# Mamba layer: side work on TensorE one matmul at a time, from two rows with one PSUM bank each

## The chip, the core and the metric

The kernel runs on one core of a Trainium2 chip. A core has TensorE (PE: matrix products into PSUM, an accumulator memory of eight banks), VectorE (DVE), ScalarE (ACT) and GpSimd (POOL) for elementwise work, and SyncE (SP), which here issues the DMAs. Each engine works through its own queue in order and waits on semaphores. The metric is the device time of one execution in microseconds (us); lower is better.

## The reference

Four layers follow each other on an input of 2 images of 256 channels and 48x48 = 2304 positions. The change touches only the first, a bidirectional Mamba layer. For each image: layer norm and a position table; an input projection to `xi` and `z` of 512 channels each; and then for each direction `s` (forward `f`, backward `b`):

```
xs    = silu(conv4(xi) + conv_b)               # depthwise, 4 taps
proj  = xs @ xproj_w.T                         # 16 values for dt, 16 B, 16 C
dt    = softplus(proj[:, :16] @ dtproj_w.T + dt_b)
h_t   = exp(dt_t * A) * h_(t-1) + dt_t * xs_t * B_t     # 512 channels x 16 states
y_t   = sum over the 16 states of h_t * C_t, plus xs_t * D
out_s = y * silu(z)
```

The two directions' sums are added, multiplied with silu(z), projected back to 256 channels and added to the input. The later layers (attention and convolutions, a graph gate with experts, a mixture of experts) are left out here.

## The kernel before

**Pieces and tiles.** The 2304 positions are cut into six chunks of 384. A *piece* is one chunk of one image in one direction: 24 pieces, in the order image 0 forward, image 0 backward, image 1 forward, image 1 backward (pieces 0 to 5, 6 to 11, 12 to 17, 18 to 23). A piece has 64 *state tiles*: 16 states times 4 blocks of 128 channels. `layer0` walks over them one by one, tile `k`, and issues for each:

- `decay(k + 4)`: ScalarE, `he = exp(dt * A)` (L573).
- `turn_b(k + 2)`: TensorE, three 128x128 transposes of `dbt` (dt, xs and B multiplied, positions on partitions) into a bank `db`, one of three (L583). `dbt` itself is made by GpSimd two groups of four tiles ahead (`scale_b`, L563).
- the scan of tile `k` on VectorE: it reads `he` and `db` (L678 forward, L680 backward). In three groups out of four it writes `ho`, and after every second tile GpSimd multiplies the pair with C into `hcp` (L687); in the fourth VectorE itself does this into `hc` (L694). ScalarE keeps the last column as `state` for the next chunk.
- `add_state`, `POOL_LAG` = 8 or `DVE_LAG` = 2 tiles later: TensorE turns the product back and adds it to three open sums `y0` to `y2` in PSUM (L608).

**The sums.** `begin` opens the three sums at tile 6 of a piece with the D term (L598, twelve matmuls) and, backward, the forward sum (L593, three matmuls); `end` empties them at tile 5 of the next piece.

**Side work.** Beside the tiles run generators, each with a number of steps, a first and a last tile: `prepare` of the next piece (convolution L305, `xproj` L323, `dt` L340, softplus, transposes of `dtu` L370), `project_in` of a later chunk (layer norm, L238 and L249), `project_out` of the last backward piece (L386, L392), and, once the input projection is done (piece 10 on), `head_products` and `contexts`, which prepare later layers. After each tile every generator is advanced until it has caught up with its line:

```python
                slot = k - k0 + 1
                for e in beside:
                    steps, n_steps, s0, s1, _ = e
                    while e[4] * (s1 - s0) < n_steps * (slot - s0) and next(steps, e) is not e:
                        e[4] += 1
```

A step holds up to six matmuls; two or more generators may step in one tile. All take their banks from one ring of two (`ps`, tag `mm`). PSUM's eight banks: three `db`, two `mm`, three `y`.

**The order on the engines** is not quite that of the program: the framework's scheduler places each engine's instructions when the kernel is built, by program order and by when it reckons their inputs ready, and may move a matmul past others. So the place of each instruction is read from the built programs here, not from the source.

**Before the first tile** the chunks 0 and 1 of image 0 are projected and piece 0 is prepared, one behind the other; the other ten chunks are projected beside pieces 0 to 9.

Of the kernel before, what the change touches and what calls it, by code (L numbers as in the profile page):

```python
# [18 lines left out]
F32 = mybir.dt.float32  # L19
# [8 lines left out]
P = 128  # L28
# [135 lines left out]
def layer0(ctx, E):  # L164
# [4 lines left out]
    TILES = NS * DB  # L169
    D = DB * P  # L170
    EXP_AHEAD, DB_AHEAD, POOL_LAG, DVE_LAG = 4, 2, 8, 2
# [5 lines left out]
    ps = ctx.enter_context(tc.tile_pool(name="l0ps_s", bufs=2, space=PSUM))  # L177
# [14 lines left out]
    def bank():  # L192

        pool, tag = (ps, "mm") if scanning else (psd, "db")
        return pool.tile([P, D], F32, tag=tag, name="mm")

    def hold():

        return bank()[:, :W]

    def project_in(b, c):
# [7 lines left out]
        yield  # L209
        mp = hold()  # L210
        for k in range(2):
            nc.tensor.matmul(mp, lhsT=E.mean_c, rhs=h[:, k, :], start=k == 0, stop=k == 1)
        nc.vector.tensor_tensor(h, h, bc(mp, [P, 2, W], 1), ALU.subtract)
        sq = up.tile([P, 2, W], F32, tag="sq", name="sq")
        nc.scalar.activation(sq, h, AF.Square)
        yield
        vp = hold()
        for k in range(2):
            nc.tensor.matmul(vp, lhsT=E.mean_c, rhs=sq[:, k, :], start=k == 0, stop=k == 1)
        rs = up.tile([P, 2 * C], F32, tag="rs", name="rs")[:, :W]  # L220
# [5 lines left out]
        yield  # L226
        nc.vector.reciprocal(rs, rs)
        yield
        nc.vector.tensor_tensor(h, h, bc(rs, [P, 2, W], 1), ALU.mult)
        for k in range(2):  # L230
            nc.vector.scalar_tensor_tensor(
                h[:, k, :], h[:, k, :], E.v("ln_g", k, 1), pos[:, k, :], ALU.mult, ALU.add
            )
        yield
        for m in range(DB):
            px = hold()
            for k in range(2):
# [3 lines left out]
                )  # L241
            xz = wp.tile([P, D], F32, tag="xz", name="xz")[:, :W]
            nc.scalar.copy(xz, px)
            nc.sync.dma_start(xi_d[b][:, m, 3 + c * W : 3 + (c + 1) * W], xz)
            yield
        for j in range(TB):
            pz = bank()
            for k in range(2):
# [3 lines left out]
                )  # L252
            xz = wp.tile([P, D], F32, tag="xz", name="xz")
            nc.scalar.copy(xz, pz)
            nc.sync.dma_start(z_d[b][:, c, j], xz)
            yield
# [34 lines left out]
    def prepare(b, s, step, c, got):  # L291
# [7 lines left out]
        yield  # L299
        xs = wp.tile([P, DB, W], F32, tag="xs", name="xs")  # L300
        for d in range(DB):
            px = hold()
            for k in range(4):
# [5 lines left out]
                if k == 1:  # L309
                    yield  # L310
# [5 lines left out]
            yield  # L316
# [3 lines left out]
        yield  # L320
        pj = hold()
        for d in range(DB):
# [3 lines left out]
            if d == 1:  # L326
                yield
# [5 lines left out]
        yield  # L333
# [4 lines left out]
        for d in range(DB):  # L338
            pd = hold()
# [5 lines left out]
            yield  # L345
        nc.scalar.activation(ex, ex, AF.Exp, scale=-1.0)
        pb = bank()
# [3 lines left out]
        yield  # L351
# [5 lines left out]
        yield  # L357
        nc.vector.tensor_tensor(dt, dt, ln, ALU.add)
        yield
# [3 lines left out]
        yield  # L363
        yield
        yield
        dtt = wp.tile([P, TB, D], F32, tag="dtt", name="dtt")
        for j in range(TB):
            pt = bank()
# [3 lines left out]
            yield  # L372
        got[-1].update(dt=dt, dtt=dtt, bt=bt)
        yield

    N_PREPARE = 27

    def project_out(b, c, yt):
# [3 lines left out]
        g = up.tile([P, DB, W], F32, tag="u", name="g")  # L382
        for j in range(TB):
            pg = bank()
# [3 lines left out]
            yield  # L388
        for m in range(2):
            po = hold()  # L390
            for d in range(DB):
# [4 lines left out]
                if d == 1:  # L396
                    yield
            nc.vector.tensor_tensor(xo[:, m, :], xo[:, m, :], po, ALU.add)
            yield
# [3 lines left out]
        yield  # L403

    N_OUT = 8

    def head_products():
# [3 lines left out]
        for h, m, z in [(h, m, z) for h in range(3) for m in range(2) for z in range(2)]:  # L411
# [8 lines left out]
            yield  # L420
            pg = ps.tile([P, 2 * C], F32, tag="mm", name="pg")
            for k in range(3):
                nc.tensor.matmul(
                    pg, lhsT=w_eo[k][:, m * P : (m + 1) * P], rhs=w_eo[k], start=k == 0, stop=k == 2
                )
            if z == 0:
# [5 lines left out]
            yield  # L432
            pu = ps.tile([P, 2 * C], F32, tag="mm", name="pu")
            for i in range(2):
                o = i * C + m * P
                for k in range(3):
# [3 lines left out]
                    )  # L440
            ub = E.ub[:, h, m, :]
# [5 lines left out]
            yield  # L447

    def contexts():
# [13 lines left out]
        yield  # L463
# [11 lines left out]
        for c in range(NCH):  # L475
            xn = normed(c)
            yield
# [6 lines left out]
            for t in range(3):  # L484
                pk = ps.tile([P, 2 * C], F32, tag="mm", name="pk")
                for k in range(2):
# [3 lines left out]
                    )  # L490
                nc.tensor.matmul(pk, lhsT=E.mean_c[0:1, :], rhs=bkv, start=False, stop=True)
                nc.scalar.activation(kv[t][0], pk[:, :C], AF.Relu)
                nc.scalar.copy(kv[t][1], pk[:, C:])
                yield
            pc = ps.tile([P, C], F32, tag="mm", name="pc")
            for m in range(2):
                ms = slice(m * P, (m + 1) * P)
                for t in range(3):
                    nc.tensor.matmul(
                        pc[:, ms], lhsT=kv[t][0][:, ms], rhs=kv[t][1][:, ms], start=t == 0, stop=t == 2  # L500
                    )
            if c == 0:
# [3 lines left out]
            yield  # L506
        cx = cx.rearrange("p (m w) -> p m w", m=2)
        nc.vector.tensor_tensor(cx, cx, bc(E.hmask, [P, 2, P], 1), ALU.mult)
        for c in range(NCH):
            xn = normed(c)  # L510
            yield
            q = up.tile([P, 2, W], F32, tag="h", name="q")
            for m in range(2):
                pq = hold()
                for k in range(2):
# [3 lines left out]
                    )  # L519
# [14 lines left out]
    for steps in (first, project_in(0, 1)):  # L534
        run(steps)
# [1703 lines left out]
```

## Time and profile before

| | |
|---|---|
| median of 3 runs | 5252.86 us (5251.17 to 5254.41) |
| the profiled execution | 5300.51 us, span 5298.4 us |
| layer 0: first scan, last scan | 110.4 us, about 2404 us |
| a piece, from its first scan to the next piece's | 92 to 105 us (piece 0: 81, piece 23: 72) |
| TensorE busy, 100 to 2400 us | 82% to 90% of each 100 us |
| VectorE busy, the same | 74% to 92% |
| GpSimd busy, the same | 80% to 98% |
| ScalarE busy, the same | 56% to 82% |

An engine's busy time counts from start to end of each instruction. TensorE's matmuls overlap in its pipeline, so its busy share says little of what it could still take; the spacing of their starts says more. An entry of the trace such as `L583 PE MATMUL db<-ident,dbt x3` is three instructions of line 583 that write `db`; `<-PE db L583` behind a time is what ended an engine's idling before it. A matmul of float32 operands shows as two records, a transpose as one.

### The profile page before, as it was taken

To read this page: it belongs to the slowest core of one execution; us is meant where nothing else is said; L and a number is where in the kernel's file an instruction comes from. 1 tells how busy PE (TensorE), PEld (TensorE's weight loads), DVE (VectorE), ACT (ScalarE), POOL (GpSimd) and SP (SyncE) were. 2 spreads that over 40 slices of the span, in tenths; PEclk is the share of its full clock that TensorE was granted. 3 is DMA by queue.
4 is the path that set the end of the run, shared out by engine and by line. 5 is a ranking of instruction groups with operands and counts; after the bars stand their busy time and mean duration, and the time that the engine had idled before them with its cause. 6 is when DMAs were issued, how large, how long until landed. Compare 5 with 4: busy or idle time off the path is not lost. (4 is left out here: it accounts for less than half of the span.)

```text
span 5298.4 us, 61375 instructions
## 1 busy us (share of the span) xinstructions
PE 4818.9 (91%) x22242; PEld 3163.5 (60%) x22242; DVE 3273.5 (62%) x4801; ACT 2416.2 (46%) x4604; POOL 2444.2 (46%) x2091
## 2 busy tenths in 40 slices
PE   7888898898888898888999999999799999999897
PEld 4666666666666666665555555566455555555675
DVE  3888878877877778888999344466524410212344
ACT  4777777766667677662232223422033322222221
POOL 2998988878888888892000000058312100000331
PEclk8999999999999999999999999999889999999899
DMA  2222222222121122213110000111021100000322
GB/s 93 73 82 79 82 84 90 91 77 83 64 75 49 60 76 77 71 61 116 40 36 32 2 17 0 48 34 28 9 96 48 48 6 6 7 9 8 81 86 97
DMA packets 156376, 294.15 MB, mean 56 GB/s; under 512 B 29495, under 2 KB 108347, under 8 KB 155804
## 3 DMA queue, kind: packets, MB, share of 16 engines
q1 hardware_dynamic: 147356, 277.37, 15.4%
q0 software_dynamic: 8704, 12.73, 1.5%
q8 instruction: 179, 2.93, 0.2%
q14 instruction: 137, 1.12, 0.1%
HBM read 211.97 MB, written 78.07 MB: 55 GB/s over the span
## 5 line engine op out<-in xcount | busy, mean ns | idle before, releaser
L687 POOL TENSOR_TENSOR hcp<-ho,cc 128x768 f32<-128x768 f32 x576 | 1067.9, 1855 | 186.6 <-DVE ho L680 101.5
L583 PE MATMUL db<-ident,dbt 128*128 128x128 f32 x4608 | 795.6, 287 | 173.4 <-DVE ho L678 63.7
L563 POOL TENSOR_SCALAR dbt<-dtt,bt 128x512 f32<-128x512 f32 x1152 | 882.8, 782 | 116.4 <-PE db L583 114.4
L583 PEld LDWEIGHTS db<-ident,dbt 128*128 128x128 f32 x4608 | 555.7, 146 | 448.9 <-issue 119.5
L608 PE MATMUL y<-ident,hcp 128*128 128x128 f32 x3456 | 570.2, 276 | 47.0 <-POOL hcp L687 46.9
L573 ACT ACTIVATE he<-dt,negab 128x384 f32<-128x384 f32 x768 | 463.5, 614 | 172.2 <-DVE ho L680 111.6
L573 ACT ACTIVATE he<-dt,negaf 128x384 f32<-128x384 f32 x768 | 460.1, 613 | 166.0 <-DVE ho L678 105.1
L680 DVE TENSOR_TENSOR_SCAN ho<-he,state,db 128x384 f32<-128x384 f32 x480 | 457.6, 998 | 117.3 <-PE db L583 95.4
L678 DVE TENSOR_TENSOR_SCAN ho<-he,state,db 128x384 f32<-128x384 f32 x480 | 456.9, 997 | 111.5 <-PE db L583 89.6
L608 PEld LDWEIGHTS y<-ident,hcp 128*128 128x128 f32 x3456 | 418.2, 142 | 56.9 <-POOL hcp L687 51.7
L2042 POOL DMA_INDIRECT xe<-xt_d,token x48 | 47.5, 990 | 757.6 <-issue 713.5
L1977 PE MATMUL po<-at,xtok 128*128 128x384 f32 x864 | 329.5, 506 | 8.2 <-ACT at L1975 8.1
L1975 ACT ACTIVATE at<-sp 128x384 f32<-128x384 f32 x216 | 104.8, 491 | 467.2 <-PE sp L1968 467.1
L1968 PE MATMUL sp<-qT,xn 128*128 128x384 f32 x864 | 317.2, 486 | 0.0
L1615 PE MATMUL ph<-xn,w 128*128 128x384 f32 x768 | 292.6, 522 | 20.7 <-issue 6.8
L1173 POOL PARTITION_ALL_REDUCE most<-most x1 | 0.4, 422 | 619.4 <-DVE most L1172 619.4
L305 PE MATMUL mm<-xw,w_cv 128*128 128x384 f32 x768 | 283.3, 493 | 0.0
L1619 ACT ACTIVATE hid<-ph,vec 128x384 f32<-128x384 f32 x192 | 110.6, 581 | 340.3 <-PE ph L1615 247.1
L904 PE MATMUL pf<-t,wfc 128*128 128x384 f32 x768 | 254.9, 487 | 2.9 <-ACT hid L908 2.8
L1977 PEld LDWEIGHTS po<-at,xtok 128*128 128x128 f32 x864 | 149.9, 189 | 177.4 <-ACT at L1975 108.4
L923 PE MATMUL po<-hid,wfc 128*128 128x384 f32 x768 | 253.6, 486 | 0.0
L1615 PEld LDWEIGHTS ph<-xn,w 128*128 128x128 f32 x768 | 148.2, 202 | 133.2 <-issue 48.6
(481 smaller groups left out, 8819.4 us busy)
## 6 DMA issues: line engine op xcount, KB each, us to landing
cc<-bcd SPq DMA_DIRECT2D x96, 768.0 KB
xw<-xi_d SPq DMA_DIRECT2D x24, 774.0 KB
w<-in_m_w SPq DMA_DIRECT2D x16, 1024.0 KB
y_d<-y SPq DMA_DIRECT2D x32, 384.0 KB
ye<-y_d SPq DMA_DIRECT2D x32, 384.0 KB
xi_d<-xz SPq DMA_DIRECT2D x48, 192.0 KB
z_d<-xz SPq DMA_DIRECT2D x36, 256.0 KB
y<-z_d SPq DMA_DIRECT2D x12, 768.0 KB
```

Of the source, the lines that this page charges most:

```text
L305: nc.tensor.matmul(px, lhsT=w_cv[b, s][:, d * 4 + k, :], rhs=xw[:, d, o : o + W], start=k == 0, stop=k == 3,)
L563: nc.gpsimd.tensor_scalar(dbt[g][:, j, :], pc["dtt"][:, j, :], pc["bt"][:, j, 16 + n : 17 + n], 1.0, ALU.mult, ALU.mult,)
L573: nc.scalar.activation(hes[k], pc["dt"][:, d, :], AF.Exp, scale=nega[pc["s"]][:, d * NS + n : d * NS + n + 1])
L583: nc.tensor.transpose(dbs[k][:, j * P : (j + 1) * P], dbt[k // DB][:, j, d * P : (d + 1) * P], E.ident)
L608: nc.tensor.matmul(pc["yt"][j][:, d * P : (d + 1) * P], lhsT=hc[:, j * P : (j + 1) * P], rhs=E.ident, is_transpose=True, start=False, stop ...
L678: nc.vector.tensor_tensor_scan(to, he, db, init, ALU.mult, ALU.add)
L680: nc.vector.tensor_tensor_scan(to[:, ::-1], he[:, ::-1], db[:, ::-1], init, ALU.mult, ALU.add)
L687: nc.gpsimd.tensor_tensor(hc, ho, bc(cc, [P, 2, W], 1), ALU.mult)
L904: nc.tensor.matmul(pf, lhsT=wfc1[:, k, f * P : (f + 1) * P], rhs=t1[:, k, :], start=k == 0, stop=k == 1,)
L1615: nc.tensor.matmul(ph, lhsT=w1[:, e, k, f * P : (f + 1) * P], rhs=xn[:, k, c * W : (c + 1) * W], start=k == 0, stop=k == 1,)
L1968: nc.tensor.matmul(sp, lhsT=xn[:, k, t0 + i * P : t0 + (i + 1) * P], rhs=qT[:, k, c * W : (c + 1) * W], start=k == 0, stop=k == 1,)
L1977: nc.tensor.matmul(po[m], lhsT=xtok[:, i, m * P : (m + 1) * P], rhs=at, start=i == 0, stop=i == MT - 1,)
```

## The change

- Side work goes in *ways*: way 0 is `prepare`, way 1 a list of `project_out`, `group_stats`, `project_in` and a portion of the head work, one behind the other. Each way has one bank of its own (`mm0`, `mm1`).
- Each generator now yields behind every matmul, with 1 (or 0.9) where a matmul was issued, and 0 where not; `advance` lets the way that lags most go on while the tile has room, and the room is 1. `prepare` has 43 steps, due at tile 54 (`READY`), where what is left of it is issued at once.
- `begin` opens one sum per tile, at tiles 8, 9 and 10, and takes that tile's room.
- `POOL_LAG` is 10 instead of 8, with seven `hcp` buffers for six; three `hc` buffers for four; `end` comes at tile 7.
- Chunk 1 is no longer projected before the first tile, but in piece 0, tiles -1 to 19; piece 1 is prepared from tile 20 on, and chunk 2 is projected in the same piece behind.

The functions changed only by added yields are shown by one example (`prepare`'s convolution):

```diff
+    READY = 54
-    EXP_AHEAD, DB_AHEAD, POOL_LAG, DVE_LAG = 4, 2, 8, 2
+    EXP_AHEAD, DB_AHEAD, POOL_LAG, DVE_LAG = 4, 2, 10, 2
-    ps = ctx.enter_context(tc.tile_pool(name="l0ps_s", bufs=2, space=PSUM))
+    ps = ctx.enter_context(tc.tile_pool(name="l0ps_s", bufs=1, space=PSUM))
...
-    def bank():
-        pool, tag = (ps, "mm") if scanning else (psd, "db")
+    def bank(way):
+        pool, tag = (ps, f"mm{way}") if scanning else (psd, "db")
         return pool.tile([P, D], F32, tag=tag, name="mm")
...
         for d in range(DB):
-            px = hold()
+            px = hold(0)
             for k in range(4):
                 o = k if fwd else 3 - k
                 nc.tensor.matmul(
                     px, lhsT=w_cv[b, s][:, d * 4 + k, :], rhs=xw[:, d, o : o + W],
                     start=k == 0, stop=k == 3,
                 )
-                if k == 1:
-                    yield
+                if k < 3:
+                    yield 1
...
             nc.scalar.activation(xs[:, d, :], px, AF.Identity, bias=E.v(f"conv_b_{s}", d, 1))
-            yield
+            yield 1
...
-    N_PREPARE = 27
+    N_PREPARE = 43
...
-    for steps in (first, project_in(0, 1)):
-        run(steps)
+    run(first)
...
-    pieces = [(0, c) for c in range(2, NCH)] + [(1, c) for c in range(NCH)]
+    pieces = [(0, c) for c in range(1, NCH)] + [(1, c) for c in range(NCH)]
...
-    def begin(pc):
-        pc["yt"] = [psy.tile([P, D], F32, tag=f"y{j}", name=f"y{j}") for j in range(TB)]
-        pc["left"] = TILES
-        for j in range(TB):
-            (matmuls of yf and D into sum j)
+    def begin(pc, j):
+        if j == 0:
+            pc["yt"] = [psy.tile([P, D], F32, tag=f"y{i}", name=f"y{i}") for i in range(TB)]
+            pc["left"] = TILES
+        (matmuls of yf and D into sum j)
+        return 1
...
+    def portion(steps, n):
+        for took in steps:
+            n -= 1
+            yield took
+            if n <= 0 and took != 1:
+                return
+
+    def advance(ways, slot, room):
+        while room > 0:
+            lags = [
+                (n_steps * (slot - s0) / (s1 - s0) - done, w)
+                for w, way in enumerate(ways) if way
+                for _, n_steps, s0, s1, done in way[:1]
+            ]
+            lag, w = max(lags, default=(0, 0))
+            if lag <= 0:
+                break
+            took = next(ways[w][0][0], ways)
+            if took is ways:
+                ways[w].pop(0)
+            else:
+                ways[w][0][4] += 1
+                room -= took or 0
+        if slot >= READY:
+            for e in ways[0]:
+                run(e[0])
+            ways[0].clear()
...
-        later.append((k0 + 6, begin, (pc,)))
-        beside = []
+        for j in range(TB):
+            later.append((k0 + 8 + j, begin, (pc, j)))
+        ways = [[], []]
+        at = 8
         if after:
-            beside.append([after, N_OUT, 6, 26, 0])
-        if i + 1 < len(order):
-            beside.append([prepare(*order[i + 1], made), N_PREPARE, 0, 53, 0])
-        if i < len(pieces):
-            beside.append([project_in(*pieces[i]), 12, 0, 62, 0])
-        elif i < len(order) - 1:
-            beside.append([islice(heads, n_late), n_late, 0, 62, 0])
-        if (b, s, step) == (1, "f", 1):
-            beside.append([group_stats(E, up, lambda: hold()[:, 0:2], 0), 3, 0, 40, 0])
+            ways[1].append([after, N_OUT, at, at + 18, 0])
+            at += 19
+        if (b, s, step) == (1, "f", 1):
+            ways[1].append([group_stats(E, up, lambda: hold(1)[:, 0:2], 0), 3, 0, 20, 0])
+            at = 20
+        if i == 0:
+            ways[1].append([project_in(*pieces[0]), N_IN, -1, 19, 0])
+            at = 20
+        if i + 1 < len(pieces):
+            ways[1].append([project_in(*pieces[i + 1]), N_IN, at, 62, 0])
+        elif i < len(order) - 1:
+            ways[1].append([portion(heads, n_late), n_late, at, 62, 0])
+        if i + 1 < len(order):
+            ways[0].append([prepare(*order[i + 1], made), N_PREPARE, 20 if i == 0 else 0, READY, 0])
...
-                        hc = wp.tile([P, 2, W], F32, tag="hcp", name="hcp", bufs=6)
+                        hc = wp.tile([P, 2, W], F32, tag="hcp", name="hcp", bufs=7)
...
-                    hc = wp.tile([P, W], F32, tag="hc", name="hc", bufs=4)
+                    hc = wp.tile([P, W], F32, tag="hc", name="hc", bufs=3)
...
+                room = 1
                 while later and later[0][0] <= k:
                     _, fn, args = later.pop(0)
-                    fn(*args)
+                    room -= fn(*args) or 0
                 slot = k - k0 + 1
-                (each generator up to its line)
+                advance(ways, slot, room)
...
-        later.append((k0 + TILES + 5, end, (pc,)))
+        later.append((k0 + TILES + 7, end, (pc,)))
```

## The prediction

> **What bounds the kernel now.** I read the parts of the page first, then the waits of 100 to 2410 us, the groups of that stretch, and the timelines of the start and of one state-tile loop. The change touches layer 0 alone, whose last scans end near 2405 us; behind them the instruction orders of the two built kernels are the same on TensorE, VectorE and GpSimd.
>
> ```profile
> engine line waited for: us in total, times, longest us
> DVE ho L680 <- PE db L583: 125.2, 91, 4.6
> ...
> POOL dbt L563 <- PE db L583: 114.4, 84, 5.8
> ...
> DVE ho L678 <- PE db L583: 106.8, 79, 3.8
> ```
>
> VectorE's scans wait 232 us for the transposed input (`db`) from TensorE; GpSimd waits for the same transposes, to get its `dbt` buffers back. No other wait of VectorE is over 17 us.
>
> ```profile
> L583 PE MATMUL db<-ident,dbt 128*128 128x128 f32 x4608 | 795.6, 287 | 173.4 <-DVE ho L678 63.7 <-DVE ho L680 46.8 <-ACT state L696 41.9
> L680 DVE TENSOR_TENSOR_SCAN ho<-he,state,db 128x384 f32<-128x384 f32 x480 | 457.6, 998 | 117.3 <-PE db L583 95.4 <-PE y L608 6.4 <-POOL hcp L687 6.2
> ```
>
> TensorE in its turn waits for the scans (the `db` ring has three banks, two tiles ahead). So neither is full: each waits for the other, in turn. The timelines of TensorE and VectorE in piece 8 show why:
>
> ```profile
> 864.61 0.49 PE L583 MATMUL db<-ident,dbt 128*128 128x128 f32 x3
> 864.93 1.02 PE L593 MATMUL y<-yf,ident 128*128 128x512 f32 x2
> 865.80 1.05 PE L598 MATMUL y<-w_db,xs 128*128 128x128 f32 x8
> 866.69 1.02 PE L593 MATMUL y<-yf,ident 128*128 128x512 f32 x2
> 867.55 1.05 PE L598 MATMUL y<-w_db,xs 128*128 128x128 f32 x8
> 868.44 1.02 PE L593 MATMUL y<-yf,ident 128*128 128x512 f32 x2
> 869.30 1.05 PE L598 MATMUL y<-w_db,xs 128*128 128x128 f32 x8
> 870.19 0.60 PE L386 MATMUL mm<-ident,y 128*128 128x128 f32 x4
> 870.63 0.49 PE L583 MATMUL db<-ident,dbt 128*128 128x128 f32 x3
> ```
> ```profile
> 871.23 1.01 DVE L680 TENSOR_TENSOR_SCAN ho<-he,state,db 128x384 f32<-128x384 f32 x1 [4.07 <-PE db L583]
> ```
>
> Opening the sums (`begin`) stands as one block of 5.3 us, with four transposes of the output projection behind it, between two `db` groups, and the scan that needs the second group comes 4.07 us late.
>
> **Prices.** From the starts of neighbouring records in these timelines: a transpose 0.109 us, so a tile's three `db` and three `y` transposes 0.65; a side matmul of 384 columns is two records of 0.323, so 0.65; of 512 columns 0.86; one of `begin`'s 128 columns 0.22. On VectorE a scan takes 0.93 of the engine (two in 1.92, with overlap), a tile that does its product on VectorE 1.48.
>
> **Part 1, one matmul per tile.** Nothing is removed or added; matmuls move. I laid the built instruction orders side by side and put the prices into each gap between two `db` groups. Over 1.31 us (a tile and one matmul) the gaps of pieces 1 to 23 hold 420 us in before and 251 in after; over 2 us, 166 and 85. What does that give? A gap hurts only where VectorE has less to do than TensorE in it, with two tiles of cover, so for each eight tiles I took the larger of the two engines' sums. Pieces 2 to 23 took 2118.7 us from first scan to first scan of the next (last scan for 23); this rule gives 1913.7 in before, so 205 (9.3 a piece) lie in waits that it does not see. In after it gives 1871.9: 41.8 less. By group, before to after: pieces 2 to 6, 419 to 420; 7 to 9, 277 to 274; 10 to 12, 276 to 260; 13 to 18, 504 to 504; 19 to 22, 363 to 341. So I expect it in the backward pieces without input projection, and almost none in 2 to 9 and 13 to 18. With stretches of sixteen tiles, as if the cover were longer, it is 81 less. With four it is 31. I take 50.
>
> Why so little: in the order of after, the first 48 tiles of a backward piece hold a matmul each, so TensorE needs 1.3 us a tile there against 0.93 to 1.48 on VectorE, while the layer norm and softplus arithmetic of VectorE (reciprocal 2.55, the others 0.8 to 2.3 each, 12 us together) all falls into tiles 46 to 50. One stretch is bound by one engine, the next by the other. What is late next, where gaps close, is TensorE itself, and close behind it GpSimd: 84 us busy of the 94 of a forward piece.
>
> **Part 2, the sums opened over three tiles.** Its block goes from 2.6 us (forward) or 5.2 (backward) to three blocks of 0.87 or 1.73. In before, the scans of tiles 8 to 11 lose 3.4 us (pieces 1 to 5) to 5.1 (19 to 22) on average, some 97 in all. Not all of it is won: TensorE's work comes back in later gaps, and the sum of part 1 has both, so nothing is added here. The product lag of 10 instead of 8, with seven buffers for six, keeps the room (14 tiles until a buffer comes round, 11 until it is read; before 12 and 9); TensorE waits 46.9 us for `hcp` in before, of which some goes: within the same sum. The three `hc` buffers for four are read two tiles later; TensorE runs ahead there; nothing. SyncE's queue holds the same DMAs; those of `project_in` and `project_out` are issued some ten tiles later, before work that is also later, and the `cc` loads keep sixteen tiles of lead; nothing, and a late `cc` would cost a few us at one place.
>
> **Part 3, the start.** Chunk 1's input projection leaves the time before the first scan.
>
> ```profile
> 36.38 2.90 PE L212 MATMUL mm<-h,mean_c 128*128 128x384 f32 x4 [5.26 <-DMA h<-in_x]
> ...
> 61.93 10.49 PE L305 MATMUL mm<-xw,w_cv 128*128 128x384 f32 x32
> ...
> 105.06 2.65 PE L370 MATMUL mm<-ident,dtu 128*128 128x128 f32 x12 [2.41 <-POOL dtu L362]
> ```
>
> The convolution (L305) starts at 61.93 behind it, and the first scan at 110.4. Its input is requested at 28.9; the load of `h` took 4.2 us from issue to use, this one is twice as large, so it can start near 35: 27 us earlier. The chunk's matmuls now stand in gaps of that chain (all but two before the `dtu` transposes), where TensorE waits for ScalarE and VectorE anyway. Given back: piece 0 holds the chunk's rest and another chunk (6 us on VectorE, 13 on TensorE, where it had 7.4 us idle), and its `dtu` transposes come at tile 61 of 64: GpSimd 3.43, turn and copy 1.0, `dbt` 0.70, three times over the three thirds with overlap, some 7 us against 4.4 of scans left. I take 9 for piece 0 and 3 for piece 1. Net 15 less; bounds 0 and 27.
>
> **Part 4, one bank per way.** The two rows of side work are `ways` in the code. A way's next group waits until ScalarE has emptied its only bank (copies of 0.56 to 0.59 us), and `db` stands queued behind that wait. Before, two banks were shared and no such wait of TensorE on ScalarE's copies is among those over 5 us. A piece opens 20 to 27 groups. Bounds: nothing, as the built order leaves a tile or the other way's matmul between most of them; and 0.56 at half of them, 6 to 7 us a piece, 150 in all. Nearest is the row of before (nothing), so I take 0, and the 150 is a rival. The Trainium skill ("Perfetto Trace Analysis", Optimization Strategy) says that one gap repeating on the engine that should be full can mean too little PSUM for the next tile, which speaks against this part. By that the 150 would be due; no run here shows it yet.
>
> **The clock.** Its granted share was 0.51 in 2300 to 2314 and 1.00 in 2362 to 2411:
>
> ```profile
> 2362.00:2411.00 49.00, 38.51 (x279) 29.78 (x278) 46.05 (x59) 24.25 (x40) 44.57 (x42) 1.00 0.09 33
> 2300.00:2314.00 14.00, 8.31 (x37) 7.11 (x38) 10.02 (x11) 6.27 (x16) 13.92 (x10) 0.51 0.18 57
> ```
>
> The first stretch is almost all transposes, the second waits for VectorE's long operations: half speed comes with idling. 188 us of pieces 1 to 22 ran at half speed, at 1.66 us a tile against 1.51: 17 us. In after TensorE has work beside most long operations; some of the 17 goes, inside the uncertainty. Were it transposes as such, stretches of seven tiles or more without a real matmul (397 tiles in before's order, 131 in after's) would run at half speed, six transposes taking 1.31 us a tile against 0.93, and after would win 266 x 0.38 = 100 more. The Trainium skill ("TensorE: Matmul & The Clock Gate", Part 4: PE-mode transpose) says that transpose mode does not count as TensorE being busy in the same way. The 1.00 over 49 us of transposes disagrees.
>
> **Sum.** The profiled execution took 5300.5 (span 5298.4), 0.9% over the median of 5252.9; 50 and 15 stay 65 at that scale. 5252.9 - 65 = 5188. 0.2%, or 10.5 us, is about what a measurement can tell from no change.
>
> **Rivals.**
> - *The unseen waits shrink too* (smaller bursts, fewer refills of the ring, fewer half-speed windows). If the 9.3 us a piece become 5: 22 x 4.3 = 95 more, 5095. For it: TensorE's waits for VectorE, each a refill. Against: the forward pieces lose most of theirs at tiles 32 to 47, beside VectorE's long operations, which stay. Chance 0.17.
> - *It is given back*: side work stands in nearly every one of the first 48 tiles, so a late scan no longer finds a tile without it to catch up in, and this costs what the opening saves. The start alone is left, or not even that: 5238 to 5260. Chance 0.13 (0.03 faster, 0.09 same, 0.01 slower).
> - *The single banks bind*: as priced, half of the openings wait out a copy; 150 less 65 is 85 slower, 5338. It decides from 65 us on, 0.12 us an opening over some 550. For it: ScalarE is 70% busy and its copy stands in order behind a state copy that waits for a scan. Against: where that scan is late, TensorE is not the bound. Chance 0.18.
> - *Half speed wherever there are only transposes*: 100 more, 5088. Chance 0.02, for the row of 1.00.
>
> **Numbers.** Forecast chance 0.50, range of its own 5140 to 5225. The range over all: below, to most of the first rival, 5100; above, to the milder half of the bank rival, 5275. Faster: 0.50 + 0.17 + 0.02 + 0.03 = 0.72; same 0.09; slower 0.19.
>
> **What would show it.** First scan near 84 us; the gap of 5.3 us at the opening gone; waits of the scans for `db` down from 232 to about 170; pieces 10 to 12 and 19 to 22 shorter by about 5 us each, 2 to 6 and 13 to 18 by under 2. Wrong, if waits of `mm` matmuls for `xs`, `dt`, `dtt` or `xz` copies reach tens of us (banks), or if GpSimd's `hcp` waits end VectorE's idling.

## The result, and the profile after

The changed kernel takes 5232.82 us, median of 7 runs (5226.67 to 5238.81), against 5252.86 for the kernel before in the same set of runs: ratio 0.9963, 95% interval 0.9951 to 0.9974, so 20 us faster. The forecast was 65, a time of 5188. The 5232.8 measured lie inside the wide range over all rivals (5100 to 5275), but outside the forecast's own (5140 to 5225). The profiled execution has a span of 5226.4.

One caution on absolute times. The profiled execution of before spans 5298.4; its time behind layer 0 was 2893.6 us, that of after 2845.8. Later runs of both kinds of kernel fall into the same two groups: 2844 to 2850 in the four profiled on chip 3, and 2888 to 2898 in all those on chips 0, 1 and 6. The difference goes with the chip and not with the kernel. So layer 0 is compared by its own times, and whole runs by ratios to before on the same chip; a ratio is turned into microseconds with 5252.9.

From the starts of the scans in the two traces (us; the columns after the first are pieces):

| | first scan | 0 | 1 | 2-6 | 7-9 | 10-12 | 13-18 | 19-22 | 23 | last scan ends |
|---|---|---|---|---|---|---|---|---|---|---|
| before | 110.4 | 80.7 | 94.6 | 468.0 | 302.0 | 305.8 | 578.1 | 392.7 | 72.4 | 2404.8 |
| after | 79.2 | 96.7 | 98.0 | 480.8 | 300.7 | 291.9 | 577.4 | 380.9 | 75.1 | 2380.6 |

The waits of after between 80 and 2390 us (engine, what it was about to do, whom it waited for; total, times, longest):

```profile
engine line waited for: us in total, times, longest us
...
POOL dbt L591 <- PE db L611: 141.8, 96, 8.7
DVE ho L744 <- PE db L611: 138.7, 199, 9.2
DVE ho L746 <- PE db L611: 125.9, 199, 6.3
...
PE mm L387 <- POOL dtu L377: 59.7, 23, 5.5
...
PE mm L319 <- ACT xs L329: 24.6, 33, 1.5
...
PE mm L246 <- ACT xz L253: 16.8, 10, 2.1
...
PE y L637 <- POOL hcp L753: 6.1, 2, 5.6
```

The scans wait 265 us for `db` where they waited 232, in 398 waits instead of 170: more and shorter ones. The wait for `hcp` is down from 46.9 to 6.1. New are waits of side matmuls (`mm`) for ScalarE's copies of the bank before. All of TensorE's `mm` waits on ScalarE together are 79.9 us in 107 waits, against 6.1 in 14 before. The groups on the page:

```profile
L611 PE MATMUL db<-ident,dbt 128*128 128x128 f32 x4608 | 794.8, 283 | 101.3 <-DVE ho L744 32.1
...
L744 DVE TENSOR_TENSOR_SCAN ho<-he,state,db 128x384 f32<-128x384 f32 x480 | 464.9, 1002 | 121.2 <-PE db L611 108.2
L746 DVE TENSOR_TENSOR_SCAN ho<-he,state,db 128x384 f32<-128x384 f32 x480 | 467.9, 1002 | 110.8 <-PE db L611 94.8
```

TensorE's idling ahead of the `db` transposes fell from 173.4 us to 101.3. The idling ahead of these two groups of scans did not fall (232.0 us, against 228.8 in the same two groups of before). The opening of the sums in piece 8 (timeline of TensorE) is now cut as the diff says:

```profile
866.17 1.02 PE L621 MATMUL y<-yf,ident 128*128 128x512 f32 x2
867.03 1.05 PE L626 MATMUL y<-w_db,xs 128*128 128x128 f32 x8
867.92 0.49 PE L611 MATMUL db<-ident,dbt 128*128 128x128 f32 x3
868.25 1.02 PE L621 MATMUL y<-yf,ident 128*128 128x512 f32 x2
869.11 1.05 PE L626 MATMUL y<-w_db,xs 128*128 128x128 f32 x8
870.00 0.49 PE L611 MATMUL db<-ident,dbt 128*128 128x128 f32 x3
```

The start, on TensorE:

```profile
33.04 10.57 PE L319 MATMUL mm<-xw,w_cv 128*128 128x384 f32 x32 [3.12 <-DMA xw<-xi_d]
...
74.20 2.25 PE L387 MATMUL mm<-ident,dtu 128*128 128x128 f32 x12
```

The convolution begins at 33.04 instead of 61.93, and the `dtu` transposes end near 76.5 instead of 107.7.

A new wait and what stands behind it, piece 3, TensorE, then ScalarE, then VectorE:

```profile
386.46 0.49 PE L611 MATMUL db<-ident,dbt 128*128 128x128 f32 x3
386.79 0.49 PE L637 MATMUL y<-ident,hcp 128*128 128x128 f32 x3
387.11 0.38 PE L611 MATMUL db<-ident,dbt 128*128 128x128 f32 x2
388.45 0.91 PE L319 MATMUL mm<-xw,w_cv 128*128 128x384 f32 x2 [0.96 <-ACT state L762]
389.20 0.27 PE L611 MATMUL db<-ident,dbt 128*128 128x128 f32 x1
```
```profile
387.31 0.61 ACT L601 ACTIVATE he<-dt,negaf 128x384 f32<-128x384 f32 x1 [0.72 <-DVE db L744]
387.84 0.56 ACT L329 ACTIVATE xs<-mm,vec 128x384 f32<-128x384 f32 x1
388.30 0.15 ACT L762 COPY state<-db 128x1 f32<-128x1 f32 x1
```
```profile
387.79 1.01 DVE L744 TENSOR_TENSOR_SCAN db<-he,state,db 128x384 f32<-128x384 f32 x1
389.51 1.02 DVE L744 TENSOR_TENSOR_SCAN ho<-he,state,db 128x384 f32<-128x384 f32 x1 [0.71 <-PE db L611]
```

Two of a tile's three `db` transposes are done, then a convolution matmul that opens a bank waits 0.96 us, until ScalarE has copied that bank out (`xs`, done at 388.40). The copy stood behind an `he` that had waited 0.72 us for a scan. The profile names the state copy behind it, which ended last. The third transpose stands behind the convolution matmul, and the scan comes 0.71 late.

### The profile page after: what moved, and what is told of

It is laid out like the page before. It is cut to its first block, busy times and chain, and to the rows that moved or that the text cites. A ratio compares the mean times of both kernels' runs of the same rounds, so it can differ in the third digit from the quotient of the medians.

```text
span 5226.4 us, 61396 instructions
## 1 busy us (share of the span) xinstructions
PE 4808.4 (92%) x22242; PEld 3138.2 (60%) x22242; DVE 3288.2 (63%) x4801; ACT 2406.3 (46%) x4600; POOL 2435.5 (47%) x2091
## 5 line engine op out<-in xcount | busy, mean ns | idle before, releaser
L591 POOL TENSOR_SCALAR dbt<-dtt,bt 128x512 f32<-128x512 f32 x1152 | 860.1, 764 | 147.1 <-PE db L611 141.8
L611 PE MATMUL db<-ident,dbt 128*128 128x128 f32 x4608 | 794.8, 283 | 101.3 <-DVE ho L744 32.1
L637 PE MATMUL y<-ident,hcp 128*128 128x128 f32 x3456 | 577.4, 276 | 6.1 <-POOL hcp L753 6.1
L744 DVE TENSOR_TENSOR_SCAN ho<-he,state,db 128x384 f32<-128x384 f32 x480 | 464.9, 1002 | 121.2 <-PE db L611 108.2
L746 DVE TENSOR_TENSOR_SCAN ho<-he,state,db 128x384 f32<-128x384 f32 x480 | 467.9, 1002 | 110.8 <-PE db L611 94.8
L319 PE MATMUL mm<-xw,w_cv 128*128 128x384 f32 x768 | 312.7, 494 | 37.2 <-ACT xs L329 24.6
L2033 PEld LDWEIGHTS sp<-qT,xn 128*128 128x128 f32 x864 | 161.6, 190 | 105.2
```

Source lines behind the costliest of these rows:

```text
L319: nc.tensor.matmul(px, lhsT=w_cv[b, s][:, d * 4 + k, :], rhs=xw[:, d, o : o + W], start=k == 0, stop=k == 3,)
L591: nc.gpsimd.tensor_scalar(dbt[g][:, j, :], pc["dtt"][:, j, :], pc["bt"][:, j, 16 + n : 17 + n], 1.0, ALU.mult, ALU.mult,)
L611: nc.tensor.transpose(dbs[k][:, j * P : (j + 1) * P], dbt[k // DB][:, j, d * P : (d + 1) * P], E.ident)
L637: nc.tensor.matmul(pc["yt"][j][:, d * P : (d + 1) * P], lhsT=hc[:, j * P : (j + 1) * P], rhs=E.ident, is_transpose=True, start=False, stop ...
L744: nc.vector.tensor_tensor_scan(to, he, db, init, ALU.mult, ALU.add)
L746: nc.vector.tensor_tensor_scan(to[:, ::-1], he[:, ::-1], db[:, ::-1], init, ALU.mult, ALU.add)
```

## The experiments

Each kernel builds on after ("the ring" is that of experiment 1) or on before, and was run in five rounds or more against before. A ratio is the time over that of before; its 95% interval stands in brackets. Differences of two ratios are uncertain by some 10 us.

**1. One ring of two banks for both rows.**
```
-ps = ctx.enter_context(tc.tile_pool(name="l0ps_s", bufs=1, space=PSUM))
+ps = ctx.enter_context(tc.tile_pool(name="l0ps_s", bufs=2, space=PSUM))
-pool, tag = (ps, f"mm{way}") if scanning else (psd, "db")
+pool, tag = (ps, "mm") if scanning else (psd, "db")
```


> The changed kernel with one ring of two banks for both ways, as in the kernel before, in place of a bank for each; all else as changed. Theory A (single banks): in the changed kernel TensorE waits some 50 us in layer 0 for ScalarE's copies out of mm (convolution 34, input projection 27), in stretches where it is the limit; where a way is alone it gets both banks here, and 25 to 45 us go: 5190 to 5208, with those waits down to under 20 us. Theory B (pace): TensorE is the limit in most of the first 48 tiles of a piece because each holds a matmul (1.3 us against 0.93 of a scan), so a matmul that waits less only waits elsewhere: 5225 to 5240, scans' waits for db still about 310 us.

Measured: 0.9914 (0.9900 to 0.9927), 45 us faster than before, 26 more than after. In its waits the copies are gone:

```profile
PE mm L387 <- POOL dtu L377: 58.7, 23, 5.6
...
PE mm L319 <- ACT xs L329: 0.3, 1, 0.3
```

All `mm` waits on ScalarE are 12.6 us in 20. So 67 us of TensorE's waits cost 26 us of time. A good part of them only changed place: TensorE's waits ahead of `db`, summed over the rows of waits, rise from 92.8 us to 133.1. The forward pieces gain most (13 to 18: 577.4 to 562.1). Theory A holds, at the upper end of its range.

**2. The sums opened in one block, in after.**
```
-later.append((k0 + 8 + j, begin, (pc, j)))
+later.append((k0 + 8, begin, (pc, j)))
```


> The changed kernel with the three sums opened in one block at tile 8 again. If the split is what earns, its block of 2.6 or 5.2 us costs what it cost before, 2 to 3 us a piece: 30 to 60 us more than the changed kernel, 5263 to 5293. Theory B: what the split saves is given back in the same piece by TensorE's pace, and undoing it costs under 15: 5233 to 5248. Theory A says the same as the first, as banks do not matter to the sums.

Measured: 0.9927 (0.9913 to 0.9940), 19 us faster than after: both theories missed. The `mm` waits on ScalarE fall to 64.9 us in 89, a part of the answer; experiments 5 and 6 look for the rest.

**3. After without the new start.** The second chunk is projected ahead of the first scan again, as in before.

> The changed kernel with the start of before: chunk 1 is projected ahead of the first tile, one chunk less beside the tiles. First scan back near 110 us, piece 0 back from 97 to about 81 us. By the profiles (31 us earlier, 16 lost in piece 0, 3 in piece 1) the start is worth 12: 5245. If all that the change won is the start, 5253, the time before.

Measured: 1.0003 (0.9994 to 1.0012). All that the change won is its start; in sum the loop won nothing.

**4. Before, the sums opened over tiles 6, 7 and 8.**
```
-later.append((k0 + 6, begin, (pc,)))
+for j in range(TB):
+    later.append((k0 + 6 + j, begin, (pc, j)))
```


> The kernel before with one edit: the three sums are opened at tiles 6, 7 and 8, one each, in place of one block at tile 6. If blocks on TensorE are what costs (the scans of tiles 8 to 11 lose 97 us in all in before), 30 to 60 us go: 5193 to 5223, more than the whole change brought. Theory B (the waits come back in the next tiles, as side work is the same): within 12 of 5253.

Measured: 1.0005 (0.9996 to 1.0014). VectorE's idling at tiles 8 to 11 (gaps between its records, mean of pieces 1 to 5) falls only from 3.4 us to 2.8. Cutting the block alone is worth nothing.

**5. Ring and block together.**

> The changed kernel with both earlier edits: side work shares one ring of two banks again (alone 5206.6), and the sums are opened in one block at tile 8 (alone 5213.2, against 5232.8 unedited). Theory A, two separate costs (a bank's copy ahead of db; the three tiles that the opening keeps): they add up, 5232.8 - 26 - 20 = 5187, range 5182 to 5193. Theory B, both edits give back the same slack (a TensorE-bound stretch): 5200 to 5208, no better than the ring alone.

Measured: 0.9930 (0.9916 to 0.9943), 37 us faster than before and 8 slower than the ring alone, which these intervals do not tell from nothing. What the block won in experiment 2 it wins only with single banks. So opening in three has no cost of its own; both theories missed.

**6. After, the openings counting as nothing in a tile's room** (`begin` without its `return 1`).

> The changed kernel, the sums still opened over tiles 8, 9 and 10, but each opening counts as nothing in the tile's room, so that side work goes on beside it. Theory A, what the opening in three costs is the room of two more tiles, by which side work ends later and beside VectorE's arithmetic: 5210 to 5218, as with one block. Theory B, it is the form (a block of 0.87 or 1.73 us in each of three tiles running, instead of one of 2.6 or 5.2): 5230 to 5250, since now a side matmul stands beside each as well.

Measured: 0.9965 (0.9952 to 0.9979), as after and at the lower end of theory B's range: the room that the openings take costs nothing. But the form that B blames costs only with single banks (experiment 5). How one block eases them, beyond the 15 us less of bank waits, stays open.

**7. Before with the new start alone.**
```
-for steps in (first, project_in(0, 1)):
-    run(steps)
+run(first)
...
+if i == 0:
+    beside.append([project_in(*pieces[0]), 12, -1, 19, 0])
-    beside.append([prepare(*order[i + 1], made), N_PREPARE, 0, 53, 0])
+beside.append([prepare(*order[i + 1], made), N_PREPARE, 20 if i == 0 else 0, 53, 0])
```
(and each later chunk's projection one piece sooner, as in after)

> The kernel before with the change's start alone: the second chunk's input projection moves behind the first scan, beside piece 0's first 19 tiles; pacing, banks and opening as before. Theory A, the start is worth what the changed kernel lost without it, 21 us, whatever the pacing: 5230, range 5225 to 5235, first scan at 79 to 84 us. Theory B, it pays only with the pacing, since the chunk's matmuls come in bursts in piece 0 otherwise and cost it more than 20 us: 5240 to 5252.

Measured: 0.9964 (0.9951 to 0.9978), 19 us, first scan at 82.4. That is theory A. With experiment 3 the start is worth 19 to 21 us from either side, whatever the pacing.

**8 and 9. Room for two matmuls in a tile** (`room = 2`), in after and with the ring.

> The changed kernel with room for two side matmuls in a tile instead of one. Theory A, the pace is what costs the loop its gain (two thirds of a piece's tiles at 1.3 us of TensorE, no tile to catch up in): a scheme that catches up in two-matmul tiles leaves more tiles free, 5215 to 5228. Theory B, the pace is what wins in the loop and the banks alone eat it: two matmuls in a tile bring back the old bursts and more waits for a bank, 5240 to 5260.

> The changed kernel with one ring of two banks (alone 0.9914 of before) and room for two side matmuls in a tile (with single banks 1.0083). Theory A, two in a tile are slow because of the single banks (a group that follows another in the same tile waits out its copy): with the ring 0.988 to 0.995. Theory B, it is the pace itself (two real matmuls in a tile are longer than the cover, and each step finds the result that it needs less ready): 1.001 to 1.008, the ring giving back only its 26 us or less.

Measured: 1.0083 (1.0069 to 1.0097) and 1.0058 (1.0045 to 1.0072); with the ring that is 76 us slower than one in a tile. The first is slower than either theory had it; the second is theory B. The ring gives back 13 here. So one in a tile is the better pace of the two, although two leave more tiles without side matmuls (by the order in the traces 20 of 64 in pieces 7 to 9, against 16, both with the ring). In pieces 7 to 9 VectorE now idles 3.4 and 3.9 us at tiles 12 to 15 and 16 to 19 (1.5 and 1.0 with one): where two matmuls stand in tile after tile, TensorE is late all along.

**10 and 11. The product lag.** With the ring: lag 8 for 10, six `hcp` and four `hc` buffers, openings and end of the sums two tiles earlier, as in before; then lag 8 with the buffers of after and openings and end one tile earlier (this edit is shown).
```
-EXP_AHEAD, DB_AHEAD, POOL_LAG, DVE_LAG = 4, 2, 10, 2
+EXP_AHEAD, DB_AHEAD, POOL_LAG, DVE_LAG = 4, 2, 8, 2
-later.append((k0 + 8 + j, begin, (pc, j)))
+later.append((k0 + 7 + j, begin, (pc, j)))
-later.append((k0 + TILES + 7, end, (pc,)))
+later.append((k0 + TILES + 6, end, (pc,)))
```


> The changed kernel with one ring of two banks, and with the product lags and buffers of before: lag 8 for 10, six hcp and four hc buffers for seven and three, and the openings and the end of the sums two tiles earlier, as that lag asks. Theory A, the prediction's: the lag is worth nothing, 0.990 to 0.993, as the ring alone. Rival, the lag is what took the 47 us of TensorE's waits for hcp away: they come back and cost a third to a half of themselves, 0.994 to 0.997.

> The changed kernel with one ring of two banks, product lag 8 for 10, and the openings and the end of the sums one tile earlier, as that lag asks; seven hcp and three hc buffers stay. With before's six and four and everything two tiles earlier it was 0.9973. Theory A, the lag itself is worth what that run lost, since products of GpSimd come less than 8 tiles ahead where it is behind: 0.996 to 0.999. Theory B, it was the six hcp buffers, which hold GpSimd back: 0.990 to 0.993.

Measured: 0.9973 (0.9964 to 0.9982) and 0.9967 (0.9955 to 0.9979): 31 and 28 us slower than the ring alone. It is not the buffers. It is the lag, or the earlier openings that come with it, which no run separates; without them the paced loop wins nothing beyond the start. The wait that grew isn't the one for `hcp`; it is (experiment 11)

```profile
PE mm L387 <- POOL dtu L377: 89.3, 23, 7.1
```

against 58.7 with lag 10.

**12. Before with the lag alone** (10, seven `hcp`, three `hc`; opening in one block, end and output projection two tiles later).

> The kernel before with the product lag of 10, seven hcp and three hc buffers, and the opening (in one block) and the end of the sums two tiles later, as that lag asks; pacing, ring and start as in before. Theory A, the lag alone wins what it won with the pacing, since TensorE's 46.9 us of waits for hcp go: 0.9935 to 0.9965. Theory B, the loop's gain needs both (bursts on TensorE still make the scans late): 0.998 to 1.001.

Measured: 0.9997 (0.9988 to 1.0006). Two of TensorE's waits in before, and the same two here:

```profile
PE mm L370 <- POOL dtu L362: 53.3, 24, 4.7
...
PE y L608 <- POOL hcp L687: 46.9, 17, 4.3
```
```profile
PE mm L370 <- POOL dtu L362: 76.3, 24, 4.3
...
PE y L608 <- POOL hcp L687: 0.4, 1, 0.4
```

The 46.9 us for `hcp` are gone, and about half of that, 23 us, turns up in the wait for `dtu`. TensorE's waits together are some 28 us less, but the scans' waits for `db` are 19 us more (246.8 to 266.0, all groups of scans). Lag without pacing wins nothing, pacing without lag wins nothing beyond the start (experiments 10 and 11 against 7), and the two together win about 26 (1 against 7).

**13 and 14. Three of the four convolution taps left out**, in before and in the ring version (the matmuls alone; the steps stay).

> The kernel before, leaving out three of the four taps of the convolution: 12 matmuls of 384 columns less in each of 24 pieces, 12 x 0.65 = 7.8 us of TensorE a piece, 179 us in the loop and 7.8 ahead of the first scan; every other instruction stays. Theory A, before is bound by turns, its side matmuls partly in gaps that TensorE waits anyway: 60 to 110 us less, 0.979 to 0.989. Theory B, TensorE is the bound wherever side work stands, in before as in the changed kernel: 130 to 187 us less, 0.964 to 0.975.

> The changed kernel with one ring of two banks, leaving out three of the four taps of the convolution (the tiles' steps as they were, 12 of them in each piece without a matmul): the same 187 us of TensorE less as in the run beside it. Theory A, spread over the tiles TensorE has become the bound in them (1.3 us a tile against 0.93 of VectorE): 120 to 187 us less than with the ring alone, 0.956 to 0.969, and 40 us or more further than the same cut does to before. Theory B, it stays bound by turns: the same saving as in before within 15 us.

Measured: 0.9786 (0.9773 to 0.9799), 112 us; and 0.9794 (0.9781 to 0.9807), 63 us beyond the ring. The first is just past theory A's range. The second is the opposite of its theory A, and misses theory B's 15 us too: of the same 187 us of TensorE, before pays 112 and the paced loop a third. So side matmuls one at a time are mostly covered, and two thirds of TensorE's work here isn't what holds the paced loop. Without the taps the two loops are alike (pieces 2 to 23: 2022.6 us and 2030.9): what the pacing wins goes with these matmuls.

**15. The next piece's row first.** With the ring; its row due by tile 46, and an empty step ends a row's turn in a tile.

> The changed kernel with one ring of two banks (alone 0.9914 of before); the next piece's row is due by tile 46 instead of 54, and an empty step ends its row's turn in a tile (not in piece 0). In the built order the softplus arithmetic then stands at tile 38 instead of 42 to 44 in pieces 13 to 18, the dtu transposes at 49 instead of 52 in pieces 7 to 9, and the layer norm's reciprocal two tiles later; the same instructions otherwise. Theory A, a part of the missing gain lies in VectorE's long operations and the transposes that wait for them: 0.985 to 0.990. Theory B, it doesn't, the order is as good as the other: 0.990 to 0.993.

Measured: 0.9908 (0.9893 to 0.9923): as the ring, theory B. Moving VectorE's long operations apart is worth nothing that these runs can tell.

**16, 17 and 18. GpSimd's `dtu` in three parts**: in before, in the ring version, and in that of experiment 15.
```
-nc.gpsimd.tensor_tensor(dtu, dt, xs, ALU.mult)
+for j in range(TB):
+    js = slice(j * P, (j + 1) * P)
+    nc.gpsimd.tensor_tensor(dtu[:, :, js], dt[:, :, js], xs[:, :, js], ALU.mult)
```


> The kernel before with GpSimd's dtu (3.43 us, once a piece) cut into three, one for each 128 columns, so that the first four transposes can start after a third; the same arithmetic. TensorE waits 53.3 us for it in all, db queued behind. Theory A, that wait is paid in full: two thirds of it go, 25 to 40 us less, 0.992 to 0.995. Theory B, before covers it (VectorE has its own long operations there): 0.997 to 1.001.

> The changed kernel with one ring of two banks (alone 0.9914), and GpSimd's dtu cut into three in the same way; TensorE waits 58.7 us for it. Theory A, the wait for dtu is what the pacing runs into: 25 to 40 us more than the ring alone, 0.984 to 0.987, and more than the same edit gives to before. Theory B, other waits take its place (VectorE's long operations stand in the same tiles): 0.989 to 0.993.

> The same cut of dtu in the version in which the next piece's row is due by tile 46 and empty steps end its turn (0.9908 without it). If waits for dtu and the clump of VectorE's long operations hide each other, so that one alone shows little, the two together give 0.980 to 0.985; if not, 0.985 to 0.992.

Measured: 0.9958 (0.9945 to 0.9972), 0.9853 (0.9838 to 0.9868) and 0.9850 (0.9835 to 0.9865). The cut wins 22 us in before, between its two theories, and 32 with the ring (theory A; the 22 and the 32 are not told apart by these intervals). That makes 77 us in all, 58 us faster than the changed kernel; with the version of 18, which is not told from it, the best here. What is cut, in the trace of the ring version without the cut (piece 8, GpSimd, then TensorE):

```profile
921.54 3.42 POOL L377 TENSOR_TENSOR dtu<-dt,xs 128x1536 f32<-128x1536 f32 x1
```
```profile
920.71 0.55 PE L611 MATMUL db<-ident,dbt 128*128 128x128 f32 x3 [0.24 <-ACT state L755]
925.02 1.97 PE L387 MATMUL mm<-ident,dtu 128*128 128x128 f32 x8 [3.77 <-POOL dtu L377]
926.79 1.06 PE L611 MATMUL db<-ident,dbt 128*128 128x128 f32 x4
```

and with it:

```profile
907.52 3.71 POOL L379 TENSOR_TENSOR dtu<-dt,xs 128x512 f32<-128x512 f32 x3
```
```profile
908.84 0.66 PE L389 MATMUL mm<-ident,dtu 128*128 128x128 f32 x4 [1.91 <-POOL dtu L379]
910.07 1.11 PE L389 MATMUL mm<-ident,dtu 128*128 128x128 f32 x4 [0.57 <-POOL dtu L379]
```

`db` stands 3.77 us behind a transpose that waits for all of `dtu`, and that starts 3.48 us after GpSimd did; with the cut it starts after 1.32 us. GpSimd does the three parts back to back in every piece, so it isn't other work of GpSimd that gets ahead. VectorE's idling at tiles 52 to 55 in pieces 7 to 9 is 6.8 us on average, and 4.3 with the cut. The row of waits itself falls less than the time does (50.0 us with the cut and the ring, against 58.7): the transposes also come one or two tiles earlier in the built order. So the chain of `dtu` is shown as the cost, the wait row alone isn't its measure.

## Why the prediction was right or wrong, point by point

**The sum.** Forecast: 50 (loop) + 15 (start) + 0 (single banks) = 65. Measured: about 25 (loop, with the banks shared) + 20 (start) - 26 (single banks) = 20, within the rounding. The two steps that failed are the price of nothing for the single banks, and the 50 for the loop, whose rule sees neither the lag nor the waits for `dtu`. That the time fell near the start's 15 is chance: a loop that won and banks that lost it again.

**The start (15): right, and a little small.** The first scan came 31.2 us earlier, not 27; piece 0 gave back 9.7 for 9 and piece 1 1.3 for 3 (after against experiment 3). 20 by the trace, 19 to 21 by the ratios.

**The single banks (0): the step that failed first.** The bound was right from both sides (nothing to 150) and the value was taken at the wrong end, because the nearest row, before's, was one of two *shared* banks: a row in which the thing priced hardly occurs (6.1 us in 14 waits). Measured against the ring: 87 more waits, 67 us, 26 us of time. The sign named for it, waits for `xs` or `xz` of tens of us, appeared. The rule of the Trainium skill ("Perfetto Trace Analysis", Optimization Strategy) spoke against this part and was right in sign here, at a sixth of the 150 set beside it. The argument against ("where that scan is late, TensorE is not the bound") fits that 67 us of waits cost 26 and not 67, but it is no reason why they would cost nothing.

**The loop (50): about half.** Pieces 2 to 23, change against before (us):

| | 2-6 | 7-9 | 10-12 | 13-18 | 19-22 | sum of 2-23 |
|---|---|---|---|---|---|---|
| by the prediction's rule | +1 | -3 | -16 | 0 | -22 | -42 |
| after | +13 | -1 | -14 | -1 | -12 | -12 |
| ring | +2 | +3 | -13 | -16 | -9 | -32 |

With the banks taken out, the rule's total is nearly met (32 of 42), and so are 2 to 6 and 10 to 12; 13 to 18 and 19 to 22 swap. Pieces 0 and 1 take another 8.4 us more than before without the new start (experiment 3), about half of it for the banks (after's two pieces against the ring's: 4.7). Taking 50 instead of the rule's 42 was the smaller slip. That the total comes near is in part luck: the rule takes whichever of TensorE and VectorE has more to do as the limit, where experiment 14 wins only a third of the work of TensorE that it takes out, and it sees no lag, without which experiments 10 and 11 win nothing in the loop.

**The lag (nothing of its own): wrong.** It was counted "within the same sum", but the rule sums each engine's work and sees no lag. In the paced loop it is worth 28 us, with the openings that go with it, which is all that the loop wins; alone it is worth nothing.

**The opening in three ("not all won, within the sum"): right, and more so than it said.** In before it wins nothing (experiment 4), and with the ring nothing that experiment 5 can tell. In the paced loop the idling at tiles 8 to 11 does go, but VectorE idles later in the piece instead. The gaps between VectorE's records in pieces 1 to 23, by the tile in which they end (us):

| tiles | 0-7 | 8-11 | 12-35 | 36-63 | all |
|---|---|---|---|---|---|
| before | 46 | 98 | 159 | 95 | 398 |
| after | 20 | 28 | 160 | 167 | 375 |
| ring | 13 | 8 | 136 | 202 | 359 |
| ring, `dtu` in three | 13 | 9 | 138 | 166 | 326 |

So of the 96 us that after saves in the first 12 tiles, 72 come back in the last 28. The cut of `dtu` takes back 36 there, about the time that it wins.

**What is late next.** The prediction named TensorE itself. Experiments 13 and 14 bear that out for a third: the paced loop pays 63 of 187 us of TensorE's work. It left out the chain GpSimd `dtu`, transposes, `db`, which it priced for piece 0 alone ("some 7 us") though the same wait comes once for each piece of before, 53.3 us in all; cutting it is worth 32 us with the ring.

**The signs.** First scan near 84: 79.2. The block of 5.3 us at the opening is gone. Pieces 10 to 12 are shorter by 4.6 us each, as said, 19 to 22 by 3.0 instead of 5, and 2 to 6 are longer by 2.6. Waits for `db` down to about 170: they rose to 265, so this sign called the forecast wrong although TensorE's idling ahead of its `db` transposes fell by 72. That was right to read as a warning: a gain of TensorE that the scans do not see is none.

**The rivals.** *Given back* comes nearest in time (5238 to 5260, the start alone left), and the table above shows the giving back. Its reason, no free tile to catch up in, is not shown: room for two leaves more tiles free and is 76 us slower, but two matmuls in a tile may cost something of their own. *The single banks bind* was the right mechanism at a sixth of its price. *The unseen waits shrink too*: they did not; what the rule leaves unexplained in pieces 2 to 23 went from 205 us to 235 in after (2106.8 less 1871.9) and, with the same 1871.9, which was worked out for the order of after, 215 with the ring (2087.4). *Half speed wherever there are only transposes*: nothing of the 100 us showed.

**The clock.** Half speed (a granted clock of 0.5) covers 150 us of pieces 1 to 23 in after, 188 in before, and 235 in the ring version, which is the fastest of the three. So it does not set their order, and where its 85 us between after and the ring come from was not tried. It covers 270 us in experiment 11 and 184 in 17: how much of what the lag and the cut of `dtu` win comes by way of the clock was not separated.

## What to carry to other kernels

A row of the trace prices a wait only if that wait could occur in it: two shared buffers say nothing of one buffer each, and a bound whose ends are 0 and 150 should then not be settled at 0. When work on a shared in-order engine is smoothed, look for the one instruction in each round that waits for another engine's long operation (here 3.4 us of GpSimd ahead of a transpose), and cut that operation so that the first consumer can start; it was worth about as much as the whole smoothing. And try two edits that loosen the same engine together before dropping either: lag and pace, each alone, measured nothing. When a wait is removed, look where the engine that waited for it idles next: here later in the same piece.

## What the runs showed that was not expected

- 67 us of waits of TensorE for ScalarE's copies cost 26 us of time; 79.9 against 12.6 us by the rows of waits.
- The same 187 us of TensorE's work were worth 112 us in the loop with bursts and 63 in the loop with one matmul per tile.
- Half of a wait that was removed turned up at another instruction of the same engine: the 46.9 us for `hcp` fell to 0.4, the `dtu` wait rose from 53.3 to 76.3, at no change in time.
- GpSimd's product over 128 x 1536 took 3.43 us in one piece and 1.27 us for each third, 0.36 more in all, and the cut was still worth 22 to 32 us (the group in before, then in experiment 17):

```profile
L362 POOL TENSOR_TENSOR dtu<-dt,xs 128x1536 f32<-128x1536 f32 x24 | 82.4, 3432 | 93.4 <-DVE dt L360 93.4
L379 POOL TENSOR_TENSOR dtu<-dt,xs 128x512 f32<-128x512 f32 x69 | 85.5, 1265 | 11.2 <-DVE dt L375 11.2
```
